# Four graph layers on one core: engine orders written as sequences, checks inside the graph, a moved input load and a branch hint

## The chip, the core and the metric

The kernel runs on one core of a Trainium2 chip. The metric is the device time of one execution in microseconds; several executions give a median. A separate profiled execution gives the span (from the program's first recorded instruction to its last) and the trace. TensorE is called PE, VectorE DVE, ScalarE ACT, GpSimd POOL and SyncE SP, as in the profile. A queue's name has a q behind it (SPq).

## The reference

Sixteen graphs (`B` = 16) of 1024 nodes with 256 features each pass four layers. Every layer normalises the rows, cuts them at zero, runs a graph attention over one shared adjacency of 1024 x 1024 and adds the result to x:

```python
h = jnp.maximum(_layernorm(x, axis=-1), 0.0)
x = x + _L0_gnn_ref(h, adj, ...)   # likewise layers 1, 2, 3
```

Layers 0, 1 and 3 score a pair of nodes by `leaky_relu(e_src[i] + e_dst[j])`, mask by the adjacency, take a softmax over j, and multiply by the projected values. Layers 0 and 1 have one head of 256, layer 3 has four heads of 64; layer 0 ends in a relu, 1 and 3 in an elu. Layer 2 is a transformer block: eight heads of 32 with masked `softmax(q k / sqrt(32))`, a layernorm, two dense maps of 256 x 256 with a relu between, and a second layernorm.

## The kernel before

All work is in float32, with scores built in transposed form (keys on the partitions). The softmax is not shifted by its maximum; sums of the weights come from ones beside the values, or in layer 2 from extra matmuls (`sums`). For that shortcut to be safe, quantities must stay within bounds, so the kernel keeps track of some: `gat_seen` and `inv_seen` (sums and minima), `degree` (neighbours of each row) and `below` (negative entries of the adjacency). `fast_path` (L623) computes everything; at its end (L1990 to L2004) six bounds are checked on DVE, folded into one column `broken`, summed over the partitions by one matmul (L2003) and cast into an integer `bad` (L2004). `tile_gnn_kernel` (L2008) then loads `bad` into a register on every engine (L2013) and enters `general_path`, a slow and safe version, only if it is above zero (L2014). With these inputs it is zero, so each engine takes the branch past the slow version.

A stage is one layer of one batch, 64 in all. The work on a stage:

- *Way in* (`way_in`, L1106): statistics of x on DVE (L1050, L1051) or from sums on ACT (L1074), reciprocal roots on POOL (L1054, L1055, L1080, L1081), normalised rows `xn` on ACT (L1157) or DVE (L1150), transposes `tp` on PE (L1096), copied to `hT` on ACT (L1099), projections `pm` on PE (L1103).
- *Layers 0 and 1*: the row of source terms is spread over the partitions or stored to DRAM and loaded back as `r` (L1312, L1323); DVE makes the masked weights `p` from `r`, `e` and the mask (L1366); PE multiplies `av` (L1383); ACT and DVE finish (`gat_out`, L1397, with ACT's `o` at L1406).
- *Layer 3*: the same with two heads in one tile, `p` at L1445, PE column-tiled in four quarters for `acc` (L1479) and `sums` (L1503), and the turn back and the adds at L1528 to L1565; the output is stored by SP (L1578).
- *Layer 2*: row-tiled scores `sc` (L1599), exponential on ACT (L1613), mask on DVE (L1621), column-tiled values `acc` (L1630); POOL issues a DMA that adds one `pe` tile onto its pair (L1647) so that `sums` (L1660) reads one of two; then the turn back (L1679) and the dense part (`feed_forward` L1741, `finish` L1783, ACT's `y` at L1758).

The adjacency comes in eight tiles of 128 rows (`edges`, SP, L724), DVE makes `flags` of them (L1885), PE turns these (L1891) and ACT writes the `mask` (L1895). Four tiles are enough for half of the attention's queries. Inputs of batches 0 and 1 are loaded first (`load_x`, L653), batch 1 behind all eight adjacency tiles (L725).

The order of work is not that of the loops. The loops only record items: `op` (L810) takes an engine, a cost in us, a rank, the instructions to issue and what comes before. `play` (L944) then simulates the items with `forward` (L842) on six time lines and issues the instructions in the order in which they began there. There are 12,280 items. `RANKS` (L47) is a string with three characters for each, a number that says which item of an engine goes first. `choose` (L824) takes, among an engine's items that can begin within `SLACK` (0.5 us) of the earliest one, that with the lowest number. The engines themselves run what they are given strictly in that order. The checks and the branch follow after `play`, outside this order.

Of the kernel before, what the change touches and what calls it, by code (L numbers as in the profile page):

```python
# [26 lines left out]
F32 = mybir.dt.float32  # L27
# [20 lines left out]
    "#+;#TX#$I#U9#U3#&X#%h#WX#)4#Wc#&>#$b#U)##w##W$5o##o##Z##D##b#$'#$-##t##$#$:##r##y##G##Q#$F#$>#/4#$N#$R##x#%-#%^"  # L48
    "#$o#'S#'T#&F#&a#%g#&$#'%#&{##T#$|##?##@#%F#SZ##B#%+##>##S#$f##c##M##a##L##]##9##v##i##z##|##u##^#$@#$)##n#$0#$4"
    "##U#oi#-@##V#sX##F##X#$^##=##_#%e##P#)h##{#$<##q#$`#/3#$&#$P##m#$3#$8#$J#$,#$9#$K#$1#*e#%r##%##j#$a#&4$0;#Cy$0r"  # L50
    "#RB#Cx#%|#']#**#&@#)g#([#'q#%m#&]#&7#%v##8#$=##}#$G##-#$L#$_#$j#$M##)#$E##p#$]$$T#'?#%a$Mo#%5#$n#$U#%L#%9#%}#%R"
    "##(#$C#%%#$c#%8##Y#&L#%7#xt#%S#'V#]n#%l#$5$%C#%V#%E#0W#%0##l#&+#$i#&,#%n#(o#)v#)V#D,#%t#$v#$r#$S#%$#%##%'#$O#$d"
    "#$H#$6#)z##4#K5#$+#&I#%?#%Y#(8#YI#(A#<Z#$A#&;#$l#%x#&1#Au#$7#(s#%,#$;#%.#%T#%z#%O#&:#DW#d-#&Q#&A#)W#%s#'H#DU#'P"
    "#'E#&0#(2#(I#(4#'r#*d#e6#&=#,6#k8#&m$Fk$Pc#($#$x#>b#$w#$Z#%3#5Q#$T#&8$@{##J#%X##O#Gr#({#%:#'K#$h#&c#'8##,#&[#%="
    "#T+#$u#&`#V9#%&#'-#%*#JZ#SB#%/#%i##C##5#%w#us##2##H##N#$s#$.#$k##e##;#$e#')#%P#&l#%<##d#$*#$##vC#%K#XB#*|#$B#%G"
    "##A$/b#&6##1#%`#&D#((#%]#%I#%{#&%##0#%_#%Q#&9#&##&)#D=##7#FF$&r#&C#%d#&.##6#)0#&B#+4#O)##3##[#&Y#%@#&g#;b$&?#e'"
    "#4O#%2#&Z#&*#(y##/#%j$/i#&&#'&#di#&p#&/#&f#&M#&|#'.#('$5w#'*#(%#&N#$2#'6#&3#&d#&R#&K#&U#&o#&V##.#DD#&E#&q#M9#'="
    "#&<#&n#eH#'D#',#w'$0(#'X#'C#&z#'J#&h#'@$6t#U@#'[#';#'A#%;#(-#'x#a}#DE#kw#'W#%p#'_#N[#&r#(>#Sm#&u#)G$.4#)P$.3#&e"
    "$Ip#'d#ma#tD#);$Pa$Ph$PQ$K?#&i#'I#&s#'N#&v#'2#&j#%A$D+#&P#&H#0A#%k#(D$JC#'p#'>#'a#&x#&_$JO#G;#O/#'5#'L#%1#'k#0>"
    "$78#(P#ip#'e#'7#kv#P)#d`$Ms$1j#'g#(G#Pd#(l#)@#(E$?$#(c#0.#'w#'s#(p#'G#)E#'}#''#(^#(&#'|#(6#UK#(/$@J#'#$@O#'y#()"  # L60
    "#ku#$Q#'v#$/#Il#.W#B1#(:#(.$>1#)3#4/#Ix#4.#(5#(L$;V$>D##k#(1$9##'u#))#(d#)%#)^#*=#)_#)t##g#'R#'j#(##(,#'U#(9#'i"
    "#(n#(B#(V#(W#&'#(*#'m#*n#)8#)1#(}#;4#)y$$:#(x#C,#(i#(Y#(h#(_#(z#)m#(U#&?#)b#(g#(k#*K#(j$*_#(f#J@#*2#)F#Ah#,[$*9"
    "#*,#*7#-z#<c#)*$LG#)=#)<#++#)M#*:#-(#(v#)B#*+#)i#:q#*1#+9#2y#)?#)Q#+J#)D$$z#*3#,,#*}#)p#)U#;Y#'h#)a#$Y#+<#*9#)S"
    "#)[#*##)$#*&#*R#+%#*H#)w#*[#,r#->#*`#+-#.S#)(#)c#)O$$u#)#$+S#s|#)R#),#/M#)+#,f#*G#+H#*p#*c#(H#*%#*E#*8$,R#*a#*4"
    "#*V#*-#+0#Q5#*k#,U#*q#+*#*@#(@$OJ#*l#-$#*j#*M#)u#qU#+N#,B#*y#K%#-g#+L#*f#*O$P,#*N#*r#+(#*_#)n#,u#j{#-'#+5#+1#IV"
    "#*o#+f#*t$3%#,k#.##h6#+?#'1#-,#,I$2J#,j#+e#L}#,b#+x#+8$2)#E7#nl#kn#+O#+##+K#-D#S{#CK#+u#Oy#)l#,*#+>#+Y$<|#+V#CP"
    "#+t#+i#.M$6O#.C#sD#,$#sv$;[#,N#+`$C?#AC#-k#?L#,'#+z#,T#:M#+D#A<#,F#,>#Os#jT#,J#00#+{#g?#+|#)r#+q#+m#+/#*]#1F#,7"
    "#/[#*U#L^#,+#q<#+X#-+#,8#.`#,3#/)$-($E##-[$F@#D$#-a$8s#Hh#-w$*S$-z#-p#.B#E##-##.u#Ob$GE#F]#+C#8u#qs#.O#.T#-u#L+"
    "#-&#.e#;g#/1#,<#.*#ej#n.#)|#j7#,}#-{#.%#-B#]z#-S#-H#-E#-G#.2#)s$#Z#.(#.c#-Z#GY#a5#/G$Ng#-b#/g$Hu#,)#.i#=.#kT#A&"
    "#gi#,&$Ch#ef$D)$Kp#,Y#8h#-f#,i#,2#-t#*<$Cj#(|#,L#,1$Cs#yr#'0#.Z#,^#8g#/U#-2#,4#'<#/##/P$MP#,o#,Z#-m#ym#2H#g=#,{"  # L70
    "#*C#/d#-O#,]#-K#+&#.-#+W#-1#,l#+o#)o#.{#,##-<#,x#-i#+S#-I#-%#/Q#+}#01#)j#-F#-3#-l#.d#*w#.K#.h$;=$/D#-`#-?$F,#.]"
    "#,X#.g#,A#-_$F)$EL$FB$A=#-o#o8#.q#.&#-N$5r$EI$FC#._#-r#-e#W[#(w#.9#)x#-d#/J$/B#-:#,Q#WZ#}i$P7#)J#-Y#-s#9m#)X#2)"
    "#-7#.N#)`#KW#-U#'l#-V#-0#,?#-x#.I#RQ#,v#/?#.>#.$#.j#.'#.A#-}#.l#/%#.V#/o#.?#-X#./#.<#.b#05#/'#``#.=#-6#'(#+h#2|"
    "#MH#-8#.7#/e#.U#g)#/f#.x#15#/s#/2#.^#,K#/I#,W#,M#Ha$P`#g[#yg#,a#/`#.v#.Y#04#/q#/;#,m#/W#.X#+v#/@#+y$K>#+r#/b#It"
    "#,s#,t$'z#0r$GX#.:#,w#,_#,z#.8#+P#-;#9-#-J#-W#Yt#.m#0S#Ys$>x$(]#.y$9$#)f#+M#$[#(r#,5#*.#*)#,P#*?#*A#,R#$W#*F#*I"
    "#*J#*Q#*>#9e#*P#)9$Kf#+6#nk#+3#+'$3l$F0#+Q#*T#,D#(`#+,#,O#(;#+$#-A#,V#h/#-.#*^#*S#*g#*{$L{#)K$3Y#)T#+a#+n#+=$)E"
    "#+I#+g#+E#+2#+[#Ba#8G#,-#>R#)6#)5#+)#-|#,@$3n#.,#.R#.6#.J$N;#.H#.G#-n#.f#;y#/$#<&#1M#]b#/5#UU#/>#.Q#.t#).#`W#]T"
    "#/Z#zN#0+#-]#*z#/m#1%#/.$7:$Nv#/}#,H#1U$EV#/O#/E#Nt#/z$(B#0&#,:#,S#*$#D5#/u#0x#C/#0i#0{$-f$Mm#-v#u'$+[#'$#0M#0L"
    "#/_##'#N<#I[#.z#3w#):#0;$?F#0(#0P$8h#NP#DY$PU#/,$@X#/t#.}#::#YZ#+R#0'#0n#/h#/v#0F#+G#/=#HG#32#03#/j#C_#/i#-j#0I"
    "#/S#18#/^#/T#3?#.5#1C#z,#HS#0?#0o#6w$-0#1A#61#1k$;Q#1$#0u#0q#/y#/<#1m#1N#0m#/B#0<#0,#2L#26#0##0l#0J#0B#14#0|#/F"  # L80
    "#0]#0V#0[$+k#0O$+f#0a#3n#.+#/D#.w#06#/p#Xr#29#0H#0%#08#0)#0G#0`#0=#0Z#0:$Nn#0y#0k#0e#1,#KY#09#0d#0z#/A#2J#fr#-9"
    "#19$8`#2a#1_#sA#1B#0h#1D#1@#2=#2b#6u#1:#1`#1G#6v#7<#/K#0X#4I$+n#0/#1T#0g#1>#1-$+`#0b#1i#1e#2E#1o#/]$8q#4H#1=#3U"
    "#1}#/c$8K#sh#s?#0K#1W$)u#2C#21#+@#1p#1;#1f#1H#A*#1Q#16#1<#1j#1I#tY$*s#2q#2I#1O#1z#2w#1x$?9#3##/(#1t#1)#1+#1?#2<"
    "#3B#3&#ZZ#2Q#1l$I6#1h#2i#1c#2B#1q#4(#2/#2j#2m#2R$K;#6(#2t#2%#1J#2x#4'#3K#2K#Y1#0t#3c#57#/n#2W$-8#2$#3N#22#1L#3)"
    "#<O#/l#2c#2;#kZ#4D#2_#5A#3M#:u#2D#4F#27#1R#2+#<N#5@#3:#2S#<z$I0$?'#3F#4C#4b#0D#88#2{$Iv#2}#0Q#3>#z0#2z$O'$O&#3$"
    "#4>#39$'1#2e#:s#3/#3j#38#3e#3=#4k#35#4=#3J#5e#3h$5E#4|#Et#+d#*;#3a#2@#5Y#4x#3b#2,#1Z#3Q#4c#4q#79#5T#5'#11#4@#4d"
    "#66#7J#5F#4S#3d#3[#4a#4?#7E$L>#7)#4p#4W#4e#5($;1#;q#6k#5)#23#3+#5$#1n#4i#5d#4^#3y#5;#5^#6H#5h#4-$>P#'B#2'#0_#6h"
    "#0*#4+#3T#3-#<6#37#<v#1a#4g$/'#2##3_#3G#=+#Kb#2Z#{?#2d#4l#nv#2[#4,#2g#4n#:t#56#3W#4J#<r$:C#5>#1b#3(#3.#4L#I=#3{"
    "#N{#3g#l?#7T#59#1^#9;#SA$Iw#2:#58#30#64#13#6Y#12#2^$/*$-7#5i#3l#3Z#8x#2F#7/#1{#*X#3v#/k#1]#8|#1($:x#3`#]k#6]#2X"
    "$JG#2O#6X#2v#3X$9<$.q#2M#07#1[#5E#@Y$)i#tL#ie#40#3C#wv#34#02#3s#T'#3I#4v#3;#3i#2P#0w#5,#2V#x^#3p#77#3O#2]#6P#5P"  # L90
    "#4M$'S#43#7'#4U#0p$,{#4*#6'#3V#3}#3o#4y#5/#2r#5o#5n#5D#6S#3S#5}#5Z#6A#4K#50#5<#67#48#5B#3L#6:#3r#3D#3]#4;#3R#6%"
    "#+j#4f#5_#^{#5H#44#5:$--#4T#33#-R#81#5V#5p#7##^$#3H#41#8;#4t#6L#5y#4m#6-#62#6W#6Q#5k$PR#7N#53#5M#$q#83#2o#5|#2p"
# [530 lines left out]
def fast_path(tc, bad, x, adj, l0_w, l0_a, l1_w, l1_a, w_qkv, ln1_g, ln1_b, ln2_g, ln2_b, w1, b1, w2, b2, l3_w, l3_a, out):  # L623
# [13 lines left out]
    with ctx:  # L637
# [306 lines left out]
        def play():  # L944
# [15 lines left out]
            for _, _, o in best[1]:  # L960
                for h in o.takes:
                    h.t = h.make(h.place) if h.ring.is_set else h.make()
                o.fn()
# [1081 lines left out]
```

## Time and profile before

| what | us |
|---|---|
| median of 3 executions (4156.73 to 4158.55) | 4158.4 |
| the profiled execution: its own time | 4158.92 |
| its span in the trace | 4157.2 |
| PE busy | 4080.8 |
| DVE busy | 3123.5 |
| ACT busy | 2316.4 |
| POOL busy | 1255.7 |

The profiled execution's own time stands 1.8 us above its span, and 0.5 above the median of the others. Busy time is a union, so a pair of overlapping matmuls counts once, and PE's busy plus its idle time make up the span. A line of waits names the waiting engine and line, what released it, the total, the number of times and the longest. In a row by stretches come the stretch, its length, and the busy time and number of instructions of PE, weight loads (PEld), DVE, ACT and POOL, then the granted clock, the DMA share and GB/s.

### The profile page before, as it was taken

How to read it: one execution, taken by the hardware profiler on the slowest of the kernel's cores; microseconds unless marked ns; L12 is line 12 of the kernel's file. 1: busy time of each engine (PE TensorE's matmuls, PEld its weight loads, DVE VectorE, ACT ScalarE, POOL GpSimd, SP SyncE). 2: the span in 40 equal slices, each digit the busy share in tenths (PEclk: the TensorE clock that was granted, in tenths of full speed). 3: DMA queues.
4: the chain of work that ended last, by engine and by line, in shares of the span. 5: the costliest groups of instructions: out<-in, count | busy, mean ns of one | idle time of the engine just before them, and what ended most of it. 6: DMA issues, size and time to landing. Idle time of an engine off the chain costs nothing. (4 is left out here: it accounts for less than half of the span.)

```text
span 4157.2 us, 67132 instructions
## 1 busy us (share of the span) xinstructions
PE 4080.8 (98%) x25993; PEld 2150.9 (52%) x25993; DVE 3123.5 (75%) x5580; ACT 2316.4 (56%) x4235; POOL 1255.7 (30%) x2153
## 2 busy tenths in 40 slices
PE   8999999999999999999999999999999999999998
PEld 7735364553646535465454654546545465465433
DVE  7477867778676886767867678686787767859697
ACT  5564655646466464654646546475564655666452
POOL 3323141413324233142322423223232232423231
PEclk9999999999999999999999999999999999999999
DMA  3181814518155181641716317163271632736361
GB/s 126 25 174 32 188 37 107 108 47 173 37 128 107 36 163 42 140 89 47 152 42 145 84 45 154 42 146 83 51 148 42 144 85 58 146 83 126 74 141 47
DMA packets 106565, 398.91 MB, mean 96 GB/s; under 512 B 11272, under 2 KB 47488, under 8 KB 73472
## 3 DMA queue, kind: packets, MB, share of 16 engines
q0 software_dynamic: 46080, 302.01, 36.8%
q1 hardware_dynamic: 59744, 92.03, 6.6%
q8 instruction: 206, 3.38, 0.3%
q14 instruction: 119, 0.97, 0.1%
q10 hardware_dynamic: 416, 0.52, 0.0%
HBM read 107.87 MB, written 18.21 MB: 30 GB/s over the span
## 5 line engine op out<-in xcount | busy, mean ns | idle before, releaser
L1621 DVE TENSOR_TENSOR pe<-pe,mask 128x1024 f32<-128x1024 f32 x1024 | 1199.7, 1219 | 198.2 <-ACT pe L1613 195.0
L1613 ACT ACTIVATE pe<-sc 128x1024 f32<-128x1024 f32 x1024 | 996.6, 1022 | 299.8 <-PE sc L1599 252.6
L1383 PE MATMUL av<-v,p 128*128 128x257 f32 x4096 | 950.4, 382 | 10.5 <-ACT o L1406 6.8
L1383 PEld LDWEIGHTS av<-v,p 128*128 128x128 f32 x4096 | 758.8, 190 | 195.6 <-issue 59.1
L1445 DVE SCALAR_TENSOR_TENSOR p<-r,e,mask 128x1024 f32<-128x1024 f32 x512 | 622.5, 1274 | 100.3 <-DMA r<-kept 94.1
L1599 PE MATMUL sc<-qT,kT 32*128 32x512 f32 x4096 | 620.0, 641 | 6.8 <-ACT pe L1613 5.3
L1630 PE MATMUL acc<-pe,v 128*32 128x512 f32 x4096 | 535.7, 604 | 2.6 <-DVE pe L1621 1.9
L1647 POOL DMA_DIRECT2D pe<-pe x256 | 226.0, 883 | 980.9 <-PE acc L1630 667.2
L1080 POOL TENSOR_SCALAR rstd<-stats 128x1 f32<-128x1 f32 x512 | 157.8, 308 | 1039.4 <-ACT xn L1074 633.6
L1479 PE MATMUL acc<-p,v 128*32 128x512 f32 x4096 | 468.1, 593 | 0.0
L1599 PEld LDWEIGHTS sc<-qT,kT 32*128 32x128 f32 x4096 | 187.6, 183 | 387.5 <-ACT pe L1613 179.9
L1103 PE MATMUL pm<-l_wx,hT 128*128 128x259 f32 (+1 forms) x1536 | 368.4, 387 | 1.3 <-DVE y L1552 0.6
L1366 DVE SCALAR_TENSOR_TENSOR p<-r,e,mask 128x512 f32<-128x512 f32 x512 | 348.6, 743 | 15.3 <-DMA r<-kept 14.4
L1081 POOL TENSOR_TENSOR rstd<-rstd,minus_half 128x1 f32<-128x1 f32 x512 | 340.1, 664 | 42.6
L1103 PEld LDWEIGHTS pm<-l_wx,hT 128*128 128x128 f32 x1536 | 285.1, 190 | 82.9 <-issue 15.1
L1054 POOL TENSOR_SCALAR rstd<-stats 128x1 f32<-128x1 f32 x256 | 148.6, 580 | 465.0 <-DVE stats L1051 459.8
L1479 PEld LDWEIGHTS acc<-p,v 128*32 128x32 f32 x4096 | 131.3, 110 | 296.3 <-issue 280.6
L1660 PE MATMUL sums<-pe,pick 128*32 128x512 f32 x2048 | 270.5, 600 | 5.6 <-DMA pe<-pe 5.4
L1630 PEld LDWEIGHTS acc<-pe,v 128*32 128x32 f32 x4096 | 96.6, 108 | 337.7 <-issue 200.1
L1157 ACT ACTIVATE xn<-x,stats 128x256 f32<-128x256 f32 x256 | 125.8, 505 | 227.9 <-DVE stats L1051 223.1
L1503 PE MATMUL sums<-p,e 128*32 128x512 f32 x2048 | 249.3, 594 | 1.4 <-ACT v L1246 0.6
L1055 POOL TENSOR_TENSOR rstd<-rstd,minus_half 128x1 f32<-128x1 f32 x256 | 232.1, 907 | 21.4
(124 smaller groups left out, 4211.6 us busy)
## 6 DMA issues: line engine op xcount, KB each, us to landing
pe<-pe POOLq DMA_DIRECT2D x256, 1024.0 KB, 8.8
r<-kept SPq DMA_DIRECT2D x64, 512.0 KB
x<-in_x_dram SPq DMA_DIRECT2D x32, 512.0 KB
x<-offsets POOLq DMA_DIRECT2D x32, 512.0 KB, 5.3
y<-offsets POOLq DMA_DIRECT2D x32, 512.0 KB, 5.9
out_dram<-x SPq DMA_DIRECT2D x64, 256.0 KB
r<-kept SPq DMA_DIRECT2D x62, 256.0 KB
edges<-in_adj_dram SPq DMA_DIRECT2D x8, 512.0 KB
```

The lines of the kernel that those rows point to most:

```text
L1081: nc.gpsimd.tensor_tensor(rh.t, rh.t, minus_half, ALU.pow)
L1103: nc.tensor.matmul(dst, lhsT=lhsT[:, k, :], rhs=rhs[:, k, :], start=(k == 0), stop=(k == KC - 1))
L1366: nc.vector.scalar_tensor_tensor(ph.t[:, j % each, :], rh.t, s.e[:, j, H + h : H + h + 1], mask[:, j, cols], ALU.max, ALU.mult)
L1383: nc.tensor.matmul(avh.t[:, : s.hs + 1], lhsT=phs[part].t[:, j % each, i * P : (i + 1) * P], rhs=s.v[:, j, h, :], start=(j == 0), stop=(j ...
L1445: nc.vector.scalar_tensor_tensor(ph.t[:, hh, :], s.rh[hp].t[:, hh, :], s.e[:, j, col : col + 1], mask[:, j, :], ALU.max, ALU.mult)
L1479: nc.tensor.matmul(acc[n].t[(2 * hh + part) * W : (2 * hh + part + 1) * W, :], lhsT=s.v[:, jj, h, part * W : (part + 1) * W], rhs=p, start ...
L1503: both(lambda jj, n, hh, h, p: nc.tensor.matmul(sums.t[(2 * n + hh) * W : (2 * n + hh + 1) * W, 0, :], lhsT=s.e[:, jj, 2 * H + h : 2 * H + ...
L1599: nc.tensor.matmul(scs[pair].t[:, hh, :], lhsT=s.kh.t[r0 : r0 + D2, g, j * P : (j + 1) * P], rhs=s.qh.t[r0 : r0 + D2, g, cols], start=True ...
L1613: lambda pair=pair: nc.scalar.activation(part(pair), scs[pair].t, AF.Exp, scale=SCALE2),
L1621: lambda pair=pair: nc.vector.tensor_tensor(part(pair), part(pair), masks(), ALU.mult), [ex], tiles=True,
L1630: nc.tensor.matmul(head(acc, i), lhsT=s.v[:, j, g * QUAD + i, :D2], rhs=ph.t[:, i, :], start=(j == 0), stop=(j == NT - 1))
L1660: nc.tensor.matmul(head(sums, i), lhsT=pick[:, g, :], rhs=th.t[:, i, :], start=first, stop=last)
```

## The change

`RANKS` is replaced by another string of 12,289 numbers (nine items more), and `forward` reads it as sequences: each engine keeps a queue of its items sorted by number, and only the head of a queue may begin. Costs of some twenty items in the planner are set anew; no instruction changes with them. The six checks, their fold and the matmul that counts them become items of the graph: each check is now one DVE instruction that compares and counts, in place of a comparison and a reduction. They depend on the items that write what they read (`seen_ops`). `load_x(1)` stands behind four adjacency tiles. When the planner's time passes 9 us before its end, a branch hint for the branch labelled "sound" is marked on all five engines; in the built program these five hints stand at the head of each engine's instructions. The string is left out here, and most of the costs:

```diff
         for t in range(NT):
             nc.sync.dma_start(out=edges[t // 2][:, t % 2, :], in_=adj[t * P : (t + 1) * P, :])
-        load_x(1)
+            if t == TH - 1:
+                load_x(1)
...
-        def forward(rank):
+        def forward(rank, in_order=True):
...
+            turns = [deque(sorted((o for o in ops if o.eng == eng), key=lambda o: rank[o.number])) for eng in range(6)]
...
             for _ in ops:
+                if in_order:
+                    open_ops = [[turn[0]] if turn and not missing[turn[0].number] else [] for turn in turns]
                 at, o = choose(open_ops, time, begin, rank, SLACK)
+                if in_order:
+                    turns[o.eng].popleft()
...
-            for _, _, o in best[1]:
+            hinted = False
+            for begun, _, o in best[1]:
+                if not hinted and begun > best[0] - HINT_AHEAD:
+                    tc.mark_branch_hint_location("sound", "LikelyTaken", engines=ENGINES)
+                    hinted = True
...
-                PE, 1.76, rank, product, [turned] + ([s.vals[0]] if ts[0] else []) + weights_in[s.layer],
+                PE, 1.775, rank, product, [turned] + ([s.vals[0]] if ts[0] else []) + weights_in[s.layer],
...
-                add = op(DVE, 0.39, rank + 0.9, add_one, [o, inv], takes=[mh], ends=[oh, ih], tiles=True)
+                add = op(DVE, 0.51, rank + 0.9, add_one, [o, inv], takes=[mh], ends=[oh, ih], tiles=True)
...
-        x_in = {b: [arrival(at) for at in places] for b, places in {0: (6.0, 7.0), 1: (21.0, 22.0)}.items()}
-        edges_in = [arrival(9.0 + 1.35 * t) for t in range(NT)]
+        x_in = {b: [arrival(at) for at in places] for b, places in {0: (5.7, 8.9), 1: (15.6, 16.9)}.items()}
+        edges_in = [arrival(10.2 + 1.28 * t + (2.7 if t >= TH else 0.0)) for t in range(NT)]
...
+        def verdict(seen_ops, checks, rank):
+
+            def count(i, seen, bound, within):
+                held = small.tile([P, 3 * B], F32, tag="held", name="held", bufs=1)[:, : seen.shape[1]]
+                nc.vector.tensor_scalar(held, seen, bound, 0.0, within, ALU.add, accum_out=ok[:, i : i + 1])
+
+            return [op(DVE, 0.26, rank + i, lambda i=i, c=c: count(i, *c), seen_ops) for i, c in checks]
...
+        def judge():
+            nc.vector.tensor_reduce(broken[:, 0:1], ok, AX.X, ALU.add)
+            nc.vector.tensor_scalar(broken[:, 0:1], broken[:, 0:1], within - 0.5, None, ALU.is_lt)
+
+        judged = op(DVE, 0.32, at - 32.0, judge, counted)
...
+        op(DVE, 0.12, at - 30.0, lambda: nc.vector.tensor_copy(bad, counth.t[:1, 0, :1]), [summed], ends=[counth])
         play()
 
 
-        checks = ((gat_seen[:, 0, :], GAT_HIGH, ALU.is_le), (gat_seen[:, 1, :], GAT_LOW, ALU.is_ge),
...
-        for i, (seen, bound, op) in enumerate(checks):
-            held = small.tile([P, 3 * B], F32, tag="held", name="held", bufs=1)[:, : seen.shape[1]]
-            nc.vector.tensor_scalar(held, seen, bound, None, op)
-            nc.vector.tensor_reduce(ok[:, i : i + 1], held, AX.X, ALU.min)
...
-        nc.tensor.matmul(count[:1, :1], lhsT=broken[:, 0:1], rhs=broken[:, 1:2], start=True, stop=True)
-        nc.vector.tensor_copy(bad, count[:1, :1])
+HINT_AHEAD = 9.0
+ENGINES = [getattr(mybir.EngineType, name) for name in ("PE", "DVE", "Activation", "Pool", "SP")]
...
-    with tc.If(found > 0):
+    with tc.If(found > 0, label="sound"):
         general_path(tc, *args)
```

## The prediction

> **What bounds the kernel now.** I read the page's head first, then TensorE's waits, then busy time by stretches, and last the end of the timeline with the instructions of the closing branch.
>
> ```profile
> span 4157.2 us, 67132 instructions
> PE 4080.8 (98%) x25993; PEld 2150.9 (52%) x25993; DVE 3123.5 (75%) x5580; ACT 2316.4 (56%) x4235; POOL 1255.7 (30%) x2153
> ```
>
> TensorE is the bound: 98% busy, with the next engine at 75%. No edit removes matmuls, so at most the idle 4157.2 - 4080.8 = 76.4 us can go, plus what is hidden inside "busy". The waits of PE (line waited for: us in total, times, longest) name most of the 76:
>
> ```profile
> PE tp L1096 <- ACT y L1758: 10.0, 8, 2.7
> PE tp L1096 <- POOL rstd L1054: 8.6, 1, 8.6
> PE count L2003 <- DVE broken L2001: 7.2, 1, 7.2
> PE av L1383 <- ACT o L1406: 6.8, 11, 1.4
> PE sums L1660 <- DMA pe<-pe: 5.4, 9, 1.9
> PE sc L1599 <- ACT pe L1613: 5.3, 6, 3.3
> PE tps L1679 <- ACT sums_sb L1670: 5.3, 5, 1.7
> ```
>
> Two are single events at the ends (8.6 at the start, 7.2 before the check). The others are many stalls of about 1 us: an item stands in PE's order too soon after the ACT or DVE work it needs. The stretches (length, then busy time of PE, PEld, DVE, ACT, POOL) say where:
>
> ```profile
> 0.00:20.00 20.00, 8.67 (x52) 7.34 (x53) 12.75 (x41) 9.84 (x14) 7.21 (x25) 1.00 0.91 329
> 4140.00:4160.00 20.00, 1.06 (x10) 0.74 (x8) 6.64 (x23) 2.47 (x5) 0.00 (x0) 0.64 0.17 57
> ```
>
> Idle in the first 20 us is 11.3. After 4140.0 it is 17.2 - 1.1 = 16.1. The middle has the rest: 76.4 - 11.3 - 16.1 = 49 us. The tail, first from the timeline (start, duration), then from the views of the branch's line and of the closing line (count: least, median and longest ns, first and last start):
>
> ```profile
> 4144.41 0.69 DVE L1565 TENSOR_TENSOR x<-x,y 128x512 f32<-128x512 f32 x1
> 4145.02 0.18 DVE L1996 TENSOR_SCALAR held<-gat_seen 128x48 f32<-128x48 f32 x1
> 4148.29 0.15 DVE L2004 CAST bad<-count 1x1 int32<-1x1 f32 x1 [0.37 <-PE count L2003]
> ```
>
> ```profile
> L2014 PEldq COMPARE_BRANCH  x1: 3475/3475/3475, 4149.1 to 4149.1; - x1
> L2041 POOLq DRAIN  x3: 40/107/6726, 4149.3 to 4156.9; - x3
> ```
>
> The last useful result is ready at T = 4144.41 + 0.69 = 4145.10. Then come 3.34 us of checks in a row on DVE (to 4148.44), a register load of `bad` on all five engines (0.5 us, L2013), the taken branch (3.5 us on PE; ACT and DVE resume at 4152.3 and 4152.7), and POOL's drain of 6.7 us, which begins only after POOL's branch. The span ends 12.05 us after T.
>
> [...] fours of column-tiled matmuls start every 0.43 us, but after the last four (about 4123.27) the 128x128 transposes start at 4123.80, 0.53 later, so a change costs about 0.1. [...] Here the last output store, issued at 4145.55, landed at 4148.89, or T + 3.8.
>
> **The change part by part.** Sums are made against the profiled span, 4157.2 (that execution took 4158.9; the median of the runs is 4158.4).
>
> *Checks in the graph and the end.* In the built program the cast of `bad` stands some 20 of the 1.28 us instructions `p` (L1445) ahead of DVE's end, about 30 us early. So 3.3 us of checks leave the tail. Two of the three waits after them are hidden too: POOL has no work after its last `rstd`, so it loads, branches and drains (0.5 + 6.7 us) under those 30 us. The check's cover is DVE's slack: before the last stage DVE waits anyway for its `r` rows (7.6 us in the chain, 4086.8 to 4094.4); without it some 2 us would show. What is late next is either the last store, T + 3.8, or DVE's own load, branch and fetch: before, 4152.85 - 4148.48 = 4.4 us, so T + 4.4. The final barrier took 4157.15 - 4156.37 = 0.8 plus 0.2 of event waits. New end: T + 5.4, a gain of 12.05 - 5.4 = 6.6. If POOL's drain cannot start early, only the checks go: 3.3. One thing is given back: in DVE's new order two adds of the previous batch (0.69 each, L1564/1565) stand between the last reciprocal and the last scaling, where 0.62 us was free: +0.8. Tail: -5.8, bounds -2.5 to -6.7.
>
> *Branch hint.* It is meant for 9 us before the end, but in the built program it is the first instruction of the kernel on every engine. No view of before shows a hint working[...]. As the store lands at T + 3.8 whatever the branch does, the whole is worth 0.4 us or less on the path. I take 0.
>
> *Second input after four adjacency tiles (SP's queue).* Two x loads of 512 KB pass four adjacency loads; at the 329 GB/s of the first row these come 1 MB or 3.2 us later, and x 2 MB earlier. The first half of the first attention needs four tiles only, but in the new DVE order seven `flags` of 1.2 us still go before the first `p`. PE's order begins transposes, projection, transposes, projection, then masks: the first projection waits for the weight columns (six of 0.42 us after six `stats`), a gap of about 2 us against 2.7 us of mask gaps before. The moved constants and the stored rows behind them have no reader for tens of us. Net 0, bounds -2 to +3.
>
> *Engine sequences.* The written sequences now hold each engine's order exactly; before, the ranks were priorities and an item that could begin within 0.5 us might go first. Either way the built order is fixed, so I compared the two built orders. Changes between column-tiled, row-tiled and full matmuls: 1532 before, 1513 after; 19 x 0.1 = -2 us. For each PE wait on an ACT, DVE or POOL result that itself waited for PE, I summed the PE work standing between, and took as need the releaser's duration (1.02 us for `pe`, 1.0 for `hT`, 0.59 for a bank's copy) plus 0.5 for two hand-overs (the tail shows 0.15 and 0.22, 0.37 together). Before, 72 of 1451 fall short, by 27.9 us together; after, 51 of 1404, by 16.3. The fold by DMA (8.8 us to land) has at least 6.7 us of PE work ahead of its reader before and 7.5 after, median 10.3 and 11.9. Stand-alone wait instructions on PE fall from 432 to 379. Shortfall is not time: 27.9 stand against 49 us of mid idle, as queues on ACT and DVE add to it. If idle scales with it, 49 x (1 - 16.3/27.9) = -20. Bounds: 0 (stalls come back at other places) to -38 (11 left). Of the edited costs in the planner none is an instruction; they only explain the order: 0.
>
> Sum: -5.8 + 0 + 0 - 2 - 20 = -28 us. 4158.4 - 28 = 4130.4.
>
> **Rivals.**
> - *Idle only moves (0.18).* The orders were improved against costs, not against the chip; other ACT and POOL queues then stall PE as before. For it: the named waits are spread over eleven kinds. Against: the shortfall falls in nearly every kind. Left: tail and changes, 4158.4 - 7.8 = 4150.6.
> - *The fit is better than I think (0.12).* Mid idle goes to 11 us and stalls hidden in "busy" go with it: 4158.4 - 7.8 - 38 = 4112.6.
> - *Slower: DVE blocked by its rows (0.05).* The PE work between the load of `r` and the first `p` that reads it falls from a median of 11.3 us to 7.8 (the shortest is 0 in both). `p` waiting at the head of DVE's queue holds the masks of `pe` behind it, and `acc` on PE behind those. DVE already waits 94.1 us in 15 places for these loads, which PE mostly does not feel. It decides when over 28 us of it come through: at 1 us more in each of 48 stages, 4158.4 - 28 + 48 = 4178.
> - *The hint does not do what it says.* True of its place; the price is 0.4 us, inside every case.
>
> **How the numbers follow.** Forecast 4130.4 with chance 0.65. The range takes in mid bounds and most of the two neighbours: low 4111, high 4151. This kernel's measurement can tell about 0.2% (8.3 us) from no change. Of the idle-only-moves case half lies within that bound: faster 0.65 + 0.12 + 0.09 = 0.86, same 0.09, slower 0.05.
>
> **What would show it.** Right: the span ends 5 to 6 us after the last x add, no checks after it, POOL's drain early; PE idle outside the first and last 20 us near 29; `sums <- DMA pe` and `tps <- sums_sb` waits reduced. Wrong: PE's middle idle still near 49, or DVE's waits for `r` above 94 us with `acc <- pe` waits grown.

## The result and the profile after

The changed kernel is slower: 4168.96 us median of 13 runs (4160.96 to 4171.77) against 4158.4 us for 13 runs of the kernel before (4153.15 to 4163.47) on the same chip. The ratio is 1.0023, 95% interval 1.0015 to 1.003, so 6 to 12 us more. The profiled execution of it took 4162.66 us, its span is 4160.9. One execution in all the runs below, of the kernel without the hint, was slow (5895 us at a mean granted clock of 0.654) and is in no ratio.

The head of the page after, to be set beside the one in the prediction:

```profile
span 4160.9 us, 66922 instructions
PE 4078.1 (98%) x25993; PEld 2161.1 (52%) x25993; DVE 3080.0 (74%) x5580; ACT 2276.2 (55%) x4235; POOL 1234.1 (30%) x2153
```

TensorE's idle time grew from 76.4 to 4160.9 - 4078.1 = 82.8 us, although the tail lost 6. TensorE's waits after (line waited for: us in total, times, longest):

```profile
PE acc L1642 <- DVE pe L1633: 9.2, 6, 7.5
PE tp L1108 <- ACT y L1770: 8.8, 2, 5.7
PE acc L1491 <- DVE p L1457: 7.0, 8, 1.9
PE av L1395 <- ACT o L1418: 5.2, 8, 2.2
PE tps L1691 <- ACT sums_sb L1682: 1.0, 2, 0.7
```

The kinds that the forecast named did fall: `tps <- sums_sb` from 5.3 to 1.0, `av <- o` from 6.8 to 5.2. But compare count and longest of the first two rows: 9.2 us in 6 waits with one of 7.5, 8.8 us in 2 waits with one of 5.7. Before, the same `tp <- y` had 10.0 us in 8, none over 2.7. Few long stalls have taken the place of many short ones.

The tail, first on the timeline, then the branch's line (engine, count, least, median and longest ns, start):

```profile
4154.62 0.69 DVE L1577 TENSOR_TENSOR x<-x,y 128x512 f32<-128x512 f32 x1
```

```profile
L2049 POOLq COMPARE_BRANCH  x1: 59/59/59, 4116.6 to 4116.6; - x1
L2049 PEldq COMPARE_BRANCH  x1: 405/405/405, 4150.3 to 4150.3; - x1
```

The last result is ready at T = 4155.31, the span ends 5.57 us later. No instruction of the checks is left there, POOL took its branch (and its drain) some 40 us early, and PE's branch fell from 3475 to 405 ns.

**Where the time went.** The two profiled executions, split in six (us). "Lost to half clock" is half of the time in the middle in which the clock's records grant 0.5 and TensorE is busy: what of such a period falls into a stall costs nothing more. Half, because the work takes twice as long there: in before the `pm` of 512 columns start 0.86 us after one another at a clock of 0.50 (3081.49 to 3083.20) and 0.43 at 1.00 (3083.74 to 3085.02). A stall counts as long from 2 us on; "work at full clock" is what is left of the time up to the last matmul of the graph.

| | before | after | difference |
|---|---|---|---|
| idle in the first 20 us | 11.3 | 9.8 | -1.5 |
| work at full clock | 4072.2 | 4060.1 | -12.1 |
| middle: stalls below 2 us | 42.9 | 37.3 | -5.6 |
| middle: stalls of 2 us and more | 6.0 (2) | 25.3 (6) | +19.3 |
| middle: lost to half clock | 8.5 | 18.0 | +9.5 |
| from the last matmul to the end | 16.3 | 10.4 | -5.9 |
| span | 4157.2 | 4160.9 | +3.7 |

The matmuls are the same (25993 in both), so I take the 12.1 us less of work at full clock, by exclusion, for stalls that don't show as idle; no view shows them. By this estimate short stalls fell by some 12.1 + 5.6 = 17.7 us, where the forecast for the middle was 22. The loss is in two rows that the forecast did not have: +19.3 and +9.5.

These two belong together: of the eight periods at half clock after, six come with one of the six long stalls. Granted clock (the column after the busy times of PE, PEld, DVE, ACT and POOL) in two stretches after and in the same two places before:

```profile
2290.00:2310.00 20.00, 14.32 (x82) 5.06 (x79) 13.56 (x16) 10.35 (x13) 13.18 (x11) 0.83 0.70 139
3800.00:3820.00 20.00, 12.54 (x57) 3.92 (x46) 10.19 (x14) 4.78 (x7) 2.13 (x3) 0.74 1.04 261
```

```profile
2290.00:2310.00 20.00, 16.74 (x88) 5.69 (x80) 13.72 (x15) 8.79 (x11) 6.87 (x7) 0.83 0.81 161
3785.00:3805.00 20.00, 20.00 (x131) 7.74 (x133) 19.73 (x27) 13.70 (x24) 8.45 (x11) 1.00 0.88 183
```

The first place is as bad before (a stall of 3.26 us); the second has no stall there at all. A clock of 0.74 over 20 us is 10.2 us at half, from 3809.05 to 3819.29. But TensorE stands still until 3814.07:

```profile
3809.00:3814.00 5.00, 0.00 (x0) 0.00 (x0) 2.54 (x4) 0.00 (x0) 0.00 (x0) 0.51 1.04 315
3814.00:3820.00 6.00, 5.93 (x21) 2.01 (x22) 6.00 (x10) 1.75 (x3) 0.85 (x1) 0.56 1.05 314
```

So only the last 5.2 us of it slow any work, and the stall of 7.46 us costs another 2.6. Some expectations below still price half of the whole period.

The profiled execution was one of the quickest of the 13. Over all runs the mean clock was 0.9935 after and, over the 46 runs of before in the first set of experiments, 0.9964. So the lower clock belongs to the kernel, not to the one profiled execution; how much of the difference fell on work, and not on stalls or on the time behind the last matmul, the means don't say.

The two longest stalls. At 3814, the timeline after (start, duration; idle before and its releaser in brackets):

```profile
3796.48 0.29 SPq L1324 DMA_DIRECT2D kept<-rows_sb  x1
3801.78 0.34 SPq L1335 DMA_DIRECT2D r<-kept  x1
3802.35 1.33 SPq L1339 DMA_DIRECT2D r<-kept  x1
...
3811.47 1.41 DVE L1378 SCALAR_TENSOR_TENSOR p<-r,e,mask 128x512 f32<-128x512 f32 x2 [9.81 <-DMA r<-kept]
3812.80 2.35 DVE L1633 TENSOR_TENSOR pe<-pe,mask 128x1024 f32<-128x1024 f32 x2
3814.07 2.20 PE L1642 MATMUL acc<-pe,v 128*32 128x512 f32 x6 [7.46 <-DVE pe L1633]
```

and the same place before:

```profile
3791.00 7.01 DVE L1621 TENSOR_TENSOR pe<-pe,mask 128x1024 f32<-128x1024 f32 x6 [0.19 <-ACT pe L1613]
3792.11 0.79 SPq L1323 DMA_DIRECT2D r<-kept  x2
3797.93 2.73 DVE L1366 SCALAR_TENSOR_TENSOR p<-r,e,mask 128x512 f32<-128x512 f32 x4
```

Before, six masks (7.01 us) cover the load of `r`. After, `p` stands first and two masks wait behind it until 3812.80, though ACT had written their inputs by 3803.95; TensorE waits behind those. The load itself is slower too: by the semaphore records of the trace the first `r` landed 9.6 us after its issue (3801.78 to 3811.37), before only 3.4 us after it (3792.11 to 3795.55). The DMA share (last column but one) in the time of the loads, before and after:

```profile
3792.00:3795.00 3.00, 3.00 (x28) 0.89 (x28) 2.98 (x4) 2.83 (x4) 0.95 (x1) 1.00 0.46 143
3802.00:3812.00 10.00, 4.61 (x16) 1.50 (x16) 0.54 (x1) 1.94 (x2) 0.00 (x0) 0.85 1.04 214
```

After, the rows share the DMA engines with two folds of 1024 KB and a transfer `y` of 512 KB, all issued by POOL; before, they were issued between two folds. Over all 126 loads of `r` the median from issue to landing is 4.95 us before and 6.44 after. So the new order asks for the rows sooner and loads them beside other traffic; no run parts the two.

At 2302 it is POOL:

```profile
2295.28 4.62 DVE L1633 TENSOR_TENSOR pe<-pe,mask 128x1024 f32<-128x1024 f32 x4
2295.37 4.61 POOL L1066 TENSOR_SCALAR rstd<-stats 128x1 f32<-128x1 f32 x1
2300.66 1.30 ACT L1770 ACTIVATE y<-y,rstd 128x256 f32<-128x256 f32 x3 [6.16 <-POOL rstd L1067]
2302.02 1.97 PE L1108 MATMUL tp<-ident,y 128*128 128x128 f32 x8 [5.68 <-ACT y L1770]
```

A POOL instruction on one column, 0.29 us in its median, takes 4.61 us, as long as four masks on DVE (4.62). It begins 0.09 us after the first of them and ends 0.08 after the last (2299.90 and 2299.98). Before has such cases too, the longest 5.30 us.

So my theory after the comparison was: the new sequences put TensorE behind two slow things, the rows `r` and POOL's root of the feed-forward's norm, in a few long stalls, and each of these halves the clock as well.

### The profile page after: what moved, and what is told of

It reads as the page before. It is cut to its first block, busy times and chain, and to the rows that moved or that the text cites. A ratio compares the mean times of both kernels' runs of the same rounds, so it can differ in the third digit from the quotient of the medians.

```text
span 4160.9 us, 66922 instructions
## 1 busy us (share of the span) xinstructions
PE 4078.1 (98%) x25993; PEld 2161.1 (52%) x25993; DVE 3080.0 (74%) x5580; ACT 2276.2 (55%) x4235; POOL 1234.1 (30%) x2153
## 5 line engine op out<-in xcount | busy, mean ns | idle before, releaser
L1457 DVE SCALAR_TENSOR_TENSOR p<-r,e,mask 128x1024 f32<-128x1024 f32 x512 | 626.1, 1272 | 111.8 <-DMA r<-kept 109.4
L1642 PE MATMUL acc<-pe,v 128*32 128x512 f32 x4096 | 548.9, 608 | 9.9 <-DVE pe L1633 9.2
L1659 POOL DMA_DIRECT2D pe<-pe x256 | 225.7, 882 | 1068.9 <-PE acc L1642 824.2
L1491 PE MATMUL acc<-p,v 128*32 128x512 f32 x4096 | 494.4, 593 | 7.0 <-DVE p L1457 7.0
L1092 POOL TENSOR_SCALAR rstd<-stats 128x1 f32<-128x1 f32 x512 | 154.3, 301 | 1006.6 <-ACT xn L1086 594.8
L1378 DVE SCALAR_TENSOR_TENSOR p<-r,e,mask 128x512 f32<-128x512 f32 x512 | 356.6, 742 | 30.5 <-DMA r<-kept 29.8
L1093 POOL TENSOR_TENSOR rstd<-rstd,minus_half 128x1 f32<-128x1 f32 x512 | 345.9, 676 | 42.6
L1066 POOL TENSOR_SCALAR rstd<-stats 128x1 f32<-128x1 f32 x256 | 141.5, 553 | 550.9 <-DVE stats L1063 539.6
L1491 PEld LDWEIGHTS acc<-p,v 128*32 128x32 f32 x4096 | 141.1, 110 | 306.4 <-issue 268.1
L1515 PE MATMUL sums<-p,e 128*32 128x512 f32 x2048 | 265.8, 593 | 1.5 <-DVE p L1457 1.4
L1412 DVE RECIPROCAL inv<-av 128x1 f32<-128x1 f32 x256 | 41.2, 163 | 276.1 <-PE av L1395 268.4
L1111 ACT ACTIVATE hT<-tp 128x1024 f32<-128x1024 f32 x160 | 163.5, 1022 | 135.3 <-PE tp L1108 134.5
```

The lines of the kernel that those rows point to most:

```text
L1093: nc.gpsimd.tensor_tensor(rh.t, rh.t, minus_half, ALU.pow)
L1378: nc.vector.scalar_tensor_tensor(ph.t[:, j % each, :], rh.t, s.e[:, j, H + h : H + h + 1], mask[:, j, cols], ALU.max, ALU.mult)
L1457: nc.vector.scalar_tensor_tensor(ph.t[:, hh, :], s.rh[hp].t[:, hh, :], s.e[:, j, col : col + 1], mask[:, j, :], ALU.max, ALU.mult)
L1491: nc.tensor.matmul(acc[n].t[(2 * hh + part) * W : (2 * hh + part + 1) * W, :], lhsT=s.v[:, jj, h, part * W : (part + 1) * W], rhs=p, start ...
L1515: both(lambda jj, n, hh, h, p: nc.tensor.matmul(sums.t[(2 * n + hh) * W : (2 * n + hh + 1) * W, 0, :], lhsT=s.e[:, jj, 2 * H + h : 2 * H + ...
L1642: nc.tensor.matmul(head(acc, i), lhsT=s.v[:, j, g * QUAD + i, :D2], rhs=ph.t[:, i, :], start=(j == 0), stop=(j == NT - 1))
```

## The experiments

Each was timed against the kernel before on the same chip; ratios are to that kernel (the change: 1.0023). Where two kernels of different sets are compared, it is by these ratios.

**The tail alone.** The order of before, with the checks as operations in the graph and the hint:

```diff
-        checks = ((gat_seen,
...
+        ok = const.tile([P, 6], F32, name="ok")
...
+                last = max(ranks[o.number] for o in seen_ops)
+                best = forward(ranks + [last + 0.1 * i for i in range(1, 10)])
...
+    with tc.If(found > 0, label="sound"):
```

> The kernel before, in its own order, with the checks in the graph and the branch hint added; no new sequences, x still loaded behind all adjacency tiles. Theory (the new sequences lose the time, the tail gains what was forecast): the end comes 5 to 6 us after the last x add instead of 12.05, nothing in the middle changes: about 4152 us, ratio 0.9985; half-clock time in the middle stays near the 17 us of before. Rival (the checks in DVE's order or the hint cost the middle): 4160 us or more.

Measured: 4160.78 us (14 runs), ratio 0.9996 (0.9987 to 1.0005). In its profile the tail is 10.5 us and the long stalls 6.0, as expected, and the profiled span is 4155.3. But the time outside the span is 3.66 to 3.96 us in all its runs, against 1.72 to 1.90 for before: 2.0 us of the 5.8 are lost outside what the profile shows. The theory's 0.9985 lies just outside the interval, and the median is in the rival's range, though no stall of the middle changed. The tail is no cause of the loss.

**The sequences alone**, with the checks after the last work, no hint, x behind all eight adjacency tiles:

```diff
-            if t == TH - 1:
-                load_x(1)
+        load_x(1)
```

> The new sequences alone: checks after the last work as before, no hint, x loaded behind all eight adjacency tiles. Theory (the sequences lose the time): as much above the changed kernel as the tail was worth, 4169 + 6 = about 4175 us, ratio 1.004, with the same long stalls of TensorE and some 44 us at half clock. Rival (one of the other three edits loses it): at or below the 4158 of before.

Measured: 4171.6 us (15 runs), ratio 1.0023 (1.0015 to 1.0031), 10 us above before. The clock's records hold 44.4 us at half clock in the middle (whole periods), as in the change, and five of its six long stalls in the middle are those of the change, at 517, 1268, 3025, 3327 and 3810. The sequences alone carry the loss, and the stalls belong to the order, not to one execution. The theory's 1.004 missed: without the other three edits the time is the same as with them (0 us, 5 either way), so the 6 us of the tail, which the spans show, don't show in the device time here either.

**Without the hint** (the call and the label taken out):

> The changed kernel without the branch hint. Theory: the end is set by the landing of the last store (T + 3.8) and what follows, so without the hint PE's branch takes 3.5 us again, and the time is 0 to 1 us longer than the changed kernel's: about 4169 to 4170 us. Rival (a hint armed from the first instruction on disturbs the fetching of instructions all through the kernel): 4160 us or less.

Measured: 4167.07 us (20 runs), ratio 1.0013 (1.0007 to 1.002). PE's branch takes 3795 ns again, the end is 6.0 us after T instead of 5.57. The rival's 4160 (a ratio of 0.9996 or less here) is excluded; the instruction queues carried no more with the hint than without it (321 packets after, 325 before). A cost of the hint of a few us is not, since the two intervals overlap; some 4 us would also fit the two runs above, in which 6 us of tail did not show. It is not shown either.

**Without the root of the feed-forward's norm:**

```diff
-            r_op = op(POOL, 1.55, rank + 0.6, root, [m_op], ends=[mh])
+            r_op = op(POOL, 1.55, rank + 0.6, root if rooted else lambda: None, [m_op], ends=[mh])
...
-                    ACT, 0.4, at + 2.0, lambda yt=yt, rh=rh: nc.scalar.activation(yt(), yt(), AF.Copy, scale=rh.t),
+                    ACT, 0.4, at + 2.0, lambda yt=yt: nc.scalar.activation(yt(), yt(), AF.Copy, scale=unit),
```

> The changed kernel without the reciprocal root of the feed-forward's norm: that part of the computation is left out (y is scaled by 1 instead), so POOL's two instructions per tile of it (L1066, L1067) are gone and ACT's scaling of y no longer waits for POOL. All orders are the same otherwise. Theory (POOL's root is kept out by runs of DVE's two-input instructions, ACT's y waits for it at the head of its queue, TensorE then stalls and its clock is halved): the stalls of 5.68, 3.81 and 3.16 us at tp <- y go (12.65 us) and with them 13.6 us at half clock (6.8 us): 4150 to 4155 us. Rival (the order on ACT is at fault, or the stall comes back at the next wait): 4165 to 4169 us.

Measured: 4148.35 us, ratio 0.997 (0.9958 to 0.9981). The three stalls at `tp <- y` are gone, those at 3020 and 3797 (the former 3814) stay, and the periods at half clock fall from 44.4 to 23.9 us. This looked like the proof of half of the theory. It was not; see the controls.

**Who suffers from POOL's late root.** The root stays on POOL, but ACT no longer reads it:

> The changed kernel in which POOL still works out the root of the feed-forward's norm, but ACT scales y by 1 and so does not wait for it (the scaling by the root is left out). Theory (the cost is ACT's wait for POOL at the head of its queue): as without the root at all, 4148 to 4152 us. Rival (POOL's work beside DVE slows DVE or the memory itself): 4162 us or more.

Measured: 4161.67 us, ratio 1.0004 (0.9996 to 1.0012), between the two. TensorE's waits say why:

```profile
PE sums L1674 <- DMA pe<-pe: 20.1, 16, 6.1
```

The root in POOL's queue has the issue of the folds by DMA (L1659) behind it. With ACT freed, TensorE waits 20.1 us in 16 places for late folds, against 6.4 us in the change itself. So a late root has two victims, and taking one away shows the other.

**The root elsewhere.** On ACT, as Ln and Exp on one column, and on DVE, as two Newton steps for four tiles at once:

```diff
+                    nc.scalar.activation(rh.t, mh.t[:, 1:2], AF.Ln, bias=eps_col)
+                    nc.scalar.activation(rh.t, rh.t, AF.Exp, scale=-0.5)
                     nc.scalar.activation(yt(), yt(), AF.Copy, scale=rh.t)
```

> The changed kernel with the same reciprocal root, worked out on ACT itself: two one-column activations (Ln, then Exp with scale -0.5) ahead of each scaling of y, with one table set that holds both loaded at the start; POOL's two instructions are gone, every other order is the same. Theory (what costs is the wait for POOL at the head of ACT's queue): as without the root, 4148 us, plus what 256 small activations on an engine that is 55% busy let through, 0 to 5 us: 4148 to 4154. Rival (leaving the root out helped because y became cheaper on ACT, not because POOL was kept out): 4162 us or more.

> The changed kernel with the same root worked out on DVE, four tiles at once behind the last one's statistics: nine instructions of 4 columns (a first guess by a shift, two Newton steps), some 0.15 us each, 32 times, so 43 us more on DVE; ACT's and POOL's other work is the same. Theory (the wait for POOL is the cost, and DVE has room): 4150 to 4160 us. Rival (the written sequences have no room for added work on DVE either): 4166 us or more.

> The changed kernel without the root (y scaled by 1; that part left out), but with the two one-column activations and the table set of the root on ACT, reading a constant and writing a column that nobody reads. Theory on why the root on ACT gave 4175 (256 small activations of 0.29 and 0.20 us, 62 us of ACT in all, ahead of y, are more than the written ACT sequence has room for): 4165 to 4176 us. Rival (the root's own wait for DVE's statistics on ACT): 4148 to 4155 us.

Measured: on ACT 4175.14 us (1.0033, 1.0021 to 1.0045), on DVE 4198.62 (1.0099, 1.0084 to 1.0115), spare activations 4155.11 (0.9989, 0.9983 to 0.9996). Both theories missed. The long stalls at `tp <- y` did go (the longest is 1.9 us in both), but stalls below 2 us rose from 37.3 to 54.8 and 52.2. ACT's busy time grew by 57.5 us against the kernel without the root (2277.3 to 2334.8) and cost 0.0063 of 4160 us, 26; DVE's by 47.0 (3079.8 to 3126.8) and cost 54. In the DVE run each scaling also waits for the statistics of all four tiles, so its 54 us are not the added work alone. The spare activations added only 34.4 (to 2311.7) and cost 8. By the number their rival was right; but they did not repeat the load that they were meant to repeat, so whether the rest on ACT is the work or the root's own wait for the statistics stays open. What is shown: in the written sequences neither place for the root was free.

In the order of before, with the tail of the change, the same root on ACT is a small gain:

> The order of before, with the checks in the graph and the hint, and the root on ACT as in the kernel beside it. Theory (the wait for POOL costs the old order too: 10.0 us in 8 waits of tp for y, of them one stall of 2.74): 4161 less 6 to 12, 4149 to 4155 us. Rival (only the new sequences meet POOL in the middle of DVE's runs): 4158 to 4162 us.

Measured: 4153.65 us (16 runs), ratio 0.9983 (0.9975 to 0.999), no long stall in the middle and 3.4 us at half clock. This version beats both kernels; against the tail alone (0.9996) its gain is 5 us, about as much as the intervals allow to tell.

**Two masks ahead of the late p** (in the changed kernel's DVE order, at 3811 us):

```diff
+                place = sorted(ranks[o.number] for o in order[first : first + 4])
+                for at, o in zip(place, order[first + 2 : first + 4] + order[first : first + 2]):
+                    ranks[o.number] = at
```

> The changed kernel with one exchange in DVE's order: the two p of L1378 that wait 9.8 us for their rows r at 3811 us now stand behind the two masks of pe (L1633) that follow them. Theory (the wait at the head of DVE's queue holds the masks back, and so TensorE): the stall of 7.46 us falls to about 2 us, since av needs the p only some 5 us later, and half-clock time falls from 10.2 to 3.4 or 6.8 us: 5.4 + 1.7 to 3.4 = 7 to 9 us less, about 4160 us. Rival (TensorE was held by something else, or waits as long for the p at av): 4167 us or more.

Measured: 4166.56 us, ratio 1.0011 (1.0003 to 1.002), not clear of the change's 1.0023. The theory failed in its size, and the profile has the reason:

```profile
3817.66 3.51 PE L1403 MATMUL av<-v,p 128*128 128x257 f32 x8 [4.07 <-DVE p L1386]
3828.73 1.23 PE L1403 MATMUL av<-v,p 128*128 128x257 f32 x2 [2.53 <-DVE p L1386]
```

`acc` no longer waits; `av` does, 4.07 + 2.53 = 6.6 of the 7.46 us. The masks behind `p` were only the first to be met: the rows themselves are too late for TensorE's order.

**No wait for rows**, and both at once:

```diff
-                        ph.t[:, j % each, :], rh.t, s.e[:, j, H + h : H + h + 1], mask[:, j, cols], ALU.max, ALU.mult
+                        ph.t[:, j % each, :], unit.to_broadcast([P, HALF]), s.e[:, j, H + h : H + h + 1], mask[:, j, cols], ALU.max, ALU.mult
```

(and the same in `pair_weights`, with N columns)

> The changed kernel in which DVE's p (L1378 and L1457) read a constant column in place of the rows r, so that they wait for no load of r (the source's share of the attention weights is left out; the loads still run). Every order is the same. Theory (the late rows hold DVE's p, the masks behind it, and TensorE): the stall of 7.46 us at 3814 with its 10.2 us at half clock goes, and most of acc's and av's waits for p, 11 us: 7.5 + 5.1 + about 7 = 12 to 20 us less than the changed kernel, 4149 to 4157 us. Rival (TensorE then meets the next late operand at the same places): 4164 us or more.

> Both at once: no root of the feed-forward's norm (y scaled by 1) and a constant in place of the rows r, so that neither POOL's root nor the loads of r can hold anything up; both parts of the computation are left out. Theory (these two causes took what the forecast of 4130 missed): 20 us from the root and 12 to 20 from the rows add up, 4128 to 4137 us. Rival (they overlap, or other stalls come in their place): 4143 us or more.

Measured: rows constant 4144.97 us, ratio 0.9954 (0.994 to 0.9967); both 4128.75, ratio 0.9912 (0.9899 to 0.9926). The rows are worth more than the 12 to 20 us expected: the stalls below 2 us fall from 37.3 to 21.9, and the work at full clock from 4060.1 to 4048.7. `p` is not cheaper itself, it only waits less; its group after and in this run (busy, mean ns | idle before it):

```profile
L1378 DVE SCALAR_TENSOR_TENSOR p<-r,e,mask 128x512 f32<-128x512 f32 x512 | 356.6, 742 | 30.5 <-DMA r<-kept 29.8
```

```profile
L1380 DVE SCALAR_TENSOR_TENSOR p<-unit,e,mask 128x512 f32<-128x512 f32 x512 | 357.0, 744 | 1.2 <-PE sc L1613 0.9 <-ACT mask L1911 0.3
```

The run also brings a stall of its own, the first of TensorE's waits in it:

```profile
PE tp L1110 <- ACT y L1155: 11.1, 1, 11.1
```

Eleven `p` that in the change wait 11.88 us for their rows at this place now follow one another at once and shut out a root on POOL for 13.22 us (shown further below). With the half clock behind it the stall costs about 14 us, an estimate from this execution: 11.1 + 6.0 / 2. So leaving the rows out shows less than the rows cost.

**The controls.** The same edits in the order of before:

> The control for the run without the root, in the order of before: the kernel before, unchanged but for the root of the feed-forward's norm, which is left out (y scaled by 1). Theory (the new sequences brought more of POOL's late roots onto TensorE's path): it gains about half of what it gained in the new sequences, 6 to 12 us, ratio 0.997 to 0.9985. Rival (both orders meet POOL alike): 18 us or more, ratio 0.9957 or less.

> The control for the constant rows, in the order of before: the kernel before with a constant column in place of the rows r (the source's share of the attention weights is left out; the loads still run). Theory (the new sequences let p wait for r where the old one did not, on TensorE's path): 4 to 12 us less, ratio 0.997 to 0.999, against 24 to 28 in the new sequences. Rival (the late rows cost the old order as much, in stalls too short to be seen): 22 us or more less, ratio 0.9947 or less.

> The control for both at once, in the order of before: no root and constant rows; both parts of the computation are left out. Theory (the new sequences are the better order once these two waits are gone, by the 22 us forecast for the middle and the 6 of the tail less what the controls say): 4142 to 4150 us, some 15 to 20 us above the same in the new sequences. Rival (both orders lose alike to the two waits): 4125 to 4135 us.

Measured, with the runs above, as ratios to the kernel before:

| | order of before | the change | what the change does to it |
|---|---|---|---|
| as it is | 1 | 1.0023 | +0.23% |
| without the root | 0.9945 (0.9932 to 0.9958) | 0.997 (0.9958 to 0.9981) | +0.25% |
| rows constant | 0.9979 (0.9971 to 0.9986) | 0.9954 (0.994 to 0.9967) | -0.25% |
| both | 0.9927 (0.9915 to 0.9939) | 0.9912 (0.9899 to 0.9926) | -0.15% |

The root costs both orders the same: 0.0055 and 0.0053 of 4160 us, 23 and 22 us. Here the rival was right, and the theory that I had formed from the long stalls fell: POOL's late root makes the longest stalls in the change and shorter ones in before, but takes as much from both. The rows cost the order of before 0.0021 x 4160 = 9 us and the change 0.0069 x 4160 = 29. These 20 us (about 7 either way, from the intervals) are what the change made dearer. If anything that is too little: constant rows bring a new stall to the order of before too, but a shorter one, 5.86 us or about 7.5 with the clock, against 14. Without rows to wait for, the change is 10 us faster than before (6 either way); without both it is 6 faster (8 either way, so not clear of nothing), and there the stall of 11.1 us stands in the change alone.

**The clock, by itself.** Bursts of matmuls with growing pauses:

> A measuring kernel: it leaves the whole computation out, copies x to the output, and runs (1) bursts of TensorE matmuls of some 30 us with pauses between them that grow from about 0.6 to 7 us in nine steps, six times over; (2) the two POOL instructions of a root beside no DVE work, and beside runs of 1, 2, 4 and 8 DVE instructions of 128x1024 with two operands in SBUF, with one, and with one in PSUM. Theory on the clock: pauses up to 1.5 us never halve the granted clock, those of 2 to 3 us in some cases, longer ones always, for 3.4 us or a multiple. [...] Theory on POOL: beside two-operand runs the root's time grows by about 1.2 us with each instruction in the run (0.9 alone, 5 or more beside four); rival: at most one instruction's length, 1.2 us, whatever the run.

```profile
820.72 36.32 PE L34 MATMUL acc<-mover,late 128*128 128x512 f32 x84 [1.46 <-DVE late L35]
859.02 35.44 PE L34 MATMUL acc<-mover,late 128*128 128x512 f32 x78 [1.98 <-DVE late L35]
```

```profile
815.00:830.00 15.00, 13.54 (x32) 5.78 (x31) 1.37 (x1) 0.00 (x0) 1.00 0.00 0
855.00:870.00 15.00, 13.02 (x27) 5.42 (x26) 1.89 (x1) 0.00 (x0) 0.89 0.00 0
```

After a pause of 1.46 us the clock stays at 1.00, after one of 1.98 it is 0.89 over 15 us: 3.4 us at half. Over the six rounds, pauses with a halved clock: none of 18 up to 1.46 us; 5 of 6 at 1.98; 2 of 6 at 2.50; 4 of 6 at 3.13; all 18 from 3.75 to 6.78. It lasts 3.4 us, from 3.13 on also 6.8, at 6.78 up to 10.2. It begins 2 to 5 us after the pause does, so that of a long pause's period a part falls into the pause; half of what falls on work is 1.4 to 3.0 us. As some pauses of 2 to 3 us halve the clock and others don't, two runs of one kernel can, as an estimate from these numbers, differ by several us with the same stalls. In the full kernels shorter recorded stalls did it too: in before 1.67 and 0.47 us at 3075 were followed by 6.8 us at half clock.

**POOL beside DVE, by itself:**

> A measuring kernel: it leaves the whole computation out, copies x to the output, and runs the two POOL instructions of a root beside runs of 1, 2, 4 and 8 DVE instructions: of two SBUF operands each on the result of the one before it (start to start 1.25 us, a small pause between), of two SBUF operands on tiles apart (as the masks of pe are), of one operand, and of one in PSUM. Theory (DVE's instructions that overlap leave POOL no moment; in the kernel they start 1.13 us after one another and last 1.22): beside runs apart, the root is done about 1.2 + 1.13 us for each further instruction later, 5 to 10 us beside 4 to 8. Rival (POOL always gets in after one instruction, as beside the chained runs, where each of its two instructions lost 0.9): at most 2.7 us for both, whatever the run.

> A measuring kernel: it leaves the whole computation out, copies x to the output, and runs POOL's two instructions of a root beside runs of 1, 2, 4 and 8 DVE instructions in the form of the masks of pe: 128x1024 of 32 bits in SBUF times a mask of 8-bit integers, repeated over two halves; for comparison the same with a mask of 32 bits repeated, with a whole second operand, and with a scalar_tensor_tensor of 256 columns. Theory (it is the form of the masks that leaves POOL no moment): beside 4 masks one POOL instruction takes 4 to 5.2 us as in the kernel, beside 8 some 9; the others let POOL in after one instruction. Rival (the form doesn't matter, something else of the full kernel does): at most 1.6 us for each of POOL's instructions in all of them.

Beside four masks in the second of them:

```profile
52.76 1.12 POOL L45 TENSOR_SCALAR root<-go 128x1 f32<-128x1 f32 x1 [0.28 <-DVE go L51]
53.97 1.40 POOL L46 TENSOR_TENSOR root<-root,half 128x1 f32<-128x1 f32 x1
```

Alone the two take 0.22 and 0.57 us. Beside runs of 2, 4 or 8 instructions of 1024 columns with two SBUF operands they take 1.1 to 1.2 and 1.4 to 1.5 us, whatever the form; beside the shorter ones of 256 columns 0.4 and 0.7, and beside an operand in PSUM 0.22 and 0.57. The rival was right in both kernels, and in the second part of the one with the bursts: each of POOL's instructions loses at most about one of DVE's, here 1.12 - 0.22 = 0.9 and 1.40 - 0.57 = 0.8 us beside masks of 1.22. In the full kernels it can lose a whole run. The longest cases are in the two runs with constant rows in the new order, where 11 `p` follow one another (here without root and rows):

```profile
1576.69 13.22 DVE L1459 SCALAR_TENSOR_TENSOR p<-unit,e,mask 128x1024 f32<-128x1024 f32 x11
1576.74 13.22 POOL L1094 TENSOR_SCALAR rstd<-stats 128x1 f32<-128x1 f32 x1 [0.59 <-ACT y L1088]
```

Of the 1536 instructions on `rstd` only 6 take over 2.7 us, before and after alike. What lets POOL in nearly always and shuts it out in these stays open.

## Why the prediction was wrong

- **Tail, -5.8: right in the span.** Measured -5.9, from the last matmul to the end. The checks' cover held, POOL's drain went early, the two adds gave back 0.6 (the last `tpv` to T: 4.24 before, 4.87 after) where 0.8 was forecast. In the device time the gain is not seen (above), and why stays open.
- **Branch hint, 0: not refuted** within the few us that the runs can tell. It does shorten PE's branch by 3.1 us, where no one waits. That this time is a fetch was my estimate: within the 3475 ns of PE's branch the trace of before has three packets on the instruction queues, within the 405 ns after none, and no view shows the branch waiting for them.
- **Second input, 0 (-2 to +3): within its bounds.** Idle in the first 20 us fell by 1.5. It was not tried alone.
- **Tiling modes and shortfall, -2 and -20: nearly right for what they count.** Short stalls fell by some 17.7 us in the profiled executions, by the estimate above. The 0.1 us for a change of the tiling is an estimate too, from one place in before (0.53 against 0.43 us); no run tests it alone.
- **The step that failed** is "If idle scales with it, 49 x (1 - 16.3/27.9) = -20. Bounds: 0 (stalls come back at other places) to -38". The count looks at one chain at a time, from TensorE over one instruction of ACT, DVE or POOL back to TensorE. It cannot see a releaser that itself waits for a DMA (`p`, 9.81 us at 3811) or is held up beside DVE's work (`rstd` on POOL, 4.61 us at 2295). Idle below 2 us followed the count, idle above it went the other way, from 6.0 to 25.3 us, and I had no term for the clock: +9.5. PE's middle idle, forecast near 29 us, is 37.3 + 25.3 = 62.6. The lower bound was wrong too: nothing kept stalls that "come back" from costing more than those that left.
- **The rival at 0.05, DVE blocked by its rows, was the case.** Its sign of recognition came true: waits of DVE for `r` rose from 94.1 + 14.4 to 109.4 + 29.8 us, and `acc <- pe` is now TensorE's first wait, with 9.2. I had its number, 11.3 us of cover falling to 7.8, and set it aside since DVE waited for `r` before as well. It came through with 20 us where 48 was the price; its threshold of 28 was wrong, because the gain that it had to eat up was smaller than 28: with the rows out of the way the change is worth 10. Its mechanism needs two corrections: not only the masks behind `p` wait, `av` needs `p` about as soon; and it is not the cover alone that shrank, since the loads also land later after their issue (6.44 against 4.95 us).
- Partly settled: why the 17.7 us of short stalls, which the sequences do save, and the tail's 6 come to only 10 even without rows. Long stalls are 34.2 us in that run and 15.7 are lost to half clock; about 14 of these 50 are the stall that constant rows bring themselves. The rest is the same trade of short stalls for long ones, by way of other waits.

## What to carry to other kernels

Stalls of TensorE are not priced alike: in the bursts a pause of up to 1.46 us cost its length, one from 1.98 us on could cost 1.4 to 3.0 us more through the clock, so a schedule that trades many short stalls for a few long ones can lose even at the same sum. When an order is tightened, look first at the readers of DMAs: a wait that an engine off the critical path already has is a cover that is used up, and the time left for the load is the number to watch, together with what else the DMA engines carry at that time (here 3.4 us to landing at a share of 0.46, 9.6 at 1.04). Leaving a wait out can make a new stall, so what such a run shows has to be looked through for stalls of its own. And a cause is tested in both kernels: without the control the root would have passed for the culprit, with 22 us and three stalls gone.

## What the runs showed of the hardware that was not expected

- Pauses of 1.98 us halved TensorE's clock (5 of 6), those of 1.46 never did (0 of 6).
- A POOL instruction on one column took 13.22 us beside 11 DVE instructions on end, which took 13.22 us together.
- A branch hint that stands as first instruction of the program still worked 4.1 ms later: 405 ns against 3475 and 3795.
- The time outside the span goes with the kernel: 1.8 us for before and after, 2.1 and 2.2 for two of the variants, 3.8 for both kernels with the order of before and the new tail; only one run of four with the root on DVE stood apart from its others (5.4 against 1.8). Nothing in the profile shows what it is.
- The half clock behind a long stall can begin inside it: 5.0 of 10.2 us at 3814, which cost nothing more.
- A 256 KB load of rows landed 3.4 us after its issue at a DMA share of 0.46, and 9.6 us after it at 1.04.
